# A decoder layer in float32: three pairs of blocks by two levels of Winograd's form in the first pass, weight preparation inside the cross-attention

## The chip, the cores and the metric

The kernel runs on one core of a Trainium2 chip. Its time is the device time of one execution in microseconds, and a comparison takes the median of several runs. The engines of the core work side by side, each through its own instructions in a fixed order: TensorE (PE in the profile, its weight loads PEld), VectorE (DVE), ScalarE (ACT), GpSimd (POOL) and SyncE (SP), which here issues most of the transfers. Transfers can also be issued from ScalarE's and GpSimd's instruction streams.

## The reference

One pre-norm decoder layer on `x` of 16 batches by 128 tokens by 1024 channels, all in float32:

```python
x = x + attn(layernorm(x), Wqkv, bqkv, Wo, bo)         # one head of 256
x = x + xattn(layernorm(x), ctx, ctx, Wq, Wk, Wv, ...)  # linear attention
x = x + ffn(layernorm(x), gate, up, down)               # int4 weights
# xattn: 8 heads of 64
qh = softmax(Wq @ q, axis=-2) * SCALE      # over a head's 64
kh = softmax(Wk @ k, axis=-1)              # over the 1024 positions
context = einsum('bhdn,bhen->bhde', kh, vh)
out = Wo @ einsum('bhde,bhdn->bhen', context, qh) + bo
out = out / max(norm(out), 1e-12) * g * sqrt(128)
# ffn: 1024 -> 2752 -> 1024, weights (nibble - zero) * scale, groups of 64
h = silu(x @ Wg.T) * (x @ Wu.T)
y = h @ Wd.T
```

## The kernel before

The program has three stages in order of time: the self-attention, the cross-attention, and the feed-forward network. The last multiplies with fewer products than the plain way: a matrix product is cut in 2 by 2 quarters and done as seven products of sums of quarters (Winograd's form of Strassen's method) instead of eight.

*Self-attention.* Four tiles of 512 tokens. Beside it, VectorE already prepares feed-forward weights.

*Weight preparation.* `prepare` (L205) is a generator that takes a list of matrices (block, and gate, up or down) and does one step at each `next`. A matrix is two halves. A step on a half is two shifts or masks that take the nibbles (`pa<-raw`), a subtraction of the zero and a multiplication by the scale, both 128x1024. After the second half comes a third step: four 128x512 combinations (`pc`) that form the sums of quarters. The seven results are stored to HBM, from where the feed-forward loads them as `w`; the stores of a step are issued by the following step, on the queue given to `prepare`. `load_raw` (L172) issues the loads of a half ahead of its step. Before, the generator `early` makes gate and up of blocks 0 to 4 in the self-attention, 30 steps, and the generator `rest` makes everything else beside the feed-forward.

*Cross-attention.* Sixteen batches, one after the other, in an order written out by hand: `key_unit` and `query_unit` alternate, and `tick()` after each counts down a list of delayed actions that `later(n, fn)` fills. So everything that follows a unit is placed a set number of ticks behind it. A query unit is two matmuls (`kq`), an exponential on ScalarE (`qe`), a row sum and reciprocal on VectorE (`qden`, `qrec`), a multiplication on GpSimd, a 32x32 transposition on VectorE (`kt`), and a trip through HBM (`kd`, `qs`) that completes the transposition. A key unit is two matmuls, an exponential (`ek`) and two matmuls with the context (`kx`). `mix` forms a batch's small matrix `m_sb`, `project_out` multiplies `qs` with it and normalises with a logarithm and an exponential on ScalarE. `kq` has two PSUM buffers, `qe` and `ek` three buffers each. `note` (L655) adds every row sum and reciprocal to running totals on GpSimd; `raise_flag` tests them at the end, for a fallback that isn't taken here. One instruction, `preload_act_table_set` at L672, loads a ScalarE table that holds logarithm and exponential together.

*Feed-forward.* The tokens are handled in two passes of eight batches. A pass multiplies its 1024 tokens with gate and up, in ten blocks of 256 rows and a smaller last block `RB`, and stores `h` to HBM; both passes' `h` are multiplied with the down weights at the end. `one_block` (L1178) does a block by one level: seven products for gate and seven for up, each four matmuls of 128x512. `two_levels` (L1360) does a pair of blocks by two levels: seven outer products, each of them seven inner products of four matmuls of 128x256, 49 in all for the 28 that two blocks take by one level. VectorE then also has to form the right operands `ti` of each outer product (`inner_right`, four operations, one outer product ahead) and to combine the results (`U`, `V`, `C`); GpSimd forms the left operands `li`. In the order of the outer products, 1, 2, 6, 5, 3, 7, 4, product 7 has the most to combine. In the second pass all five pairs go by two levels, with right operands that are kept; in the first pass only the pairs in `PAIRS` do. A step of `rest` is taken beside most products (`beside`, L1567) and after three of the seven outer products.

The order on each engine: what is wrapped in `InOrder` (L55) stays in the order of the program text, which gives all its instructions the line 63; the rest is placed by the tile framework when the program is built. A tile's buffer is reused when its last reader is done.

In the profile each float32 matmul leaves two records, so a product of four matmuls shows as x8.

Of the kernel before, what the change touches and what calls it, by code (L numbers as in the profile page):

```python
# [18 lines left out]
P = 128  # L19
# [47 lines left out]
def decoder_layer(  # L67
# [95 lines left out]
    def prep_pools(stack, name, c, ahead):  # L163
        for key, bufs in (("a", 3), ("c", c), ("raw", ahead + 1), ("sz", ahead + 1)):
            pools[key] = stack.enter_context(
                tc.tile_pool(name=f"{name}_{key}", bufs=bufs, side="right", reuse_waits="tile")
            )
# [4 lines left out]
    def load_raw(blk, mat, s):  # L172
# [3 lines left out]
        if mat == "d":  # L176
            raw, sz = raw[:w], pools["sz"].tile([P, 2, 512], F32, name="szd")[:w]
            nc.sync.dma_start(raw, dq[ds(start // 2, w), ts(s, 512)])
            for g in range(w // 32):
                row = dsz[start // GROUP + g, ts(s, 1024)].rearrange("(t f) -> t f", t=2)  # L180
                nc.sync.dma_start(sz[ts(g, 32)], row.partition_broadcast(32))
            return raw, *(sz[:, t].unsqueeze(1).to_broadcast([w, 2, 512]) for t in range(2))
# [12 lines left out]
        for m, off, w in parts:  # L195
            q, szs = matrices[m]
            nc.sync.dma_start(raw[:, :, ds(at, w)], q[:, :, ds(off, w)])
            nc.sync.dma_start(
# [6 lines left out]
    def prepare(jobs, ahead, queue, vector=nc.vector):  # L205
# [3 lines left out]
        loads = deque(load_raw(*u) for u in units[:ahead])  # L209
# [6 lines left out]
        for k, (blk, mat, s) in enumerate(units):  # L216
# [6 lines left out]
            if k + ahead < len(units):  # L223
                loads.append(load_raw(*units[k + ahead]))
# [61 lines left out]
    EARLY = 5  # L286

    def give_half(b, h, oT, wo_d, psum, tensor=nc.tensor, vector=nc.vector):
# [19 lines left out]
    prep_pools(first, "q", 4, 1)  # L308
    early = prepare(
        [(blk, mat) for blk in range(EARLY) for mat in "gu"], 1, nc.gpsimd, InOrder(tc, nc.vector)  # L310
    )
    give_pool = ExitStack()
    ag = give_pool.enter_context(tc.tile_pool(name="a_g", bufs=1, reuse_waits="tile"))
    with (
# [166 lines left out]
        for t in range(NT):  # L481
# [38 lines left out]
            else:  # L520

                for i in range(1, BPT):
                    give((t - 1) * BPT + i - 1, oT)
                    value(i, xnT, v)
                atT = turn_weights(at)
# [25 lines left out]
    def block_loads(p, blocks):  # L551

        for n, half in ((0, 0), (1, 0), (1, 1), (0, 1)):
            for i in range(2):
                src = xt_all[p][ds(half * BPT + 2 * i, 2), :, :, :, n]
                tc.keep_in_program_order(
                    nc.sync.dma_start(
# [44 lines left out]
    bcx = unit_pool("b_cx", 2)  # L602
    bw = unit_pool("b_w", 1)
    b0 = unit_pool("b_0", 2)
    bek = unit_pool("b_ek", 3)
    bas = unit_pool("b_as", 1)
    b3 = unit_pool("b_3", 3)
# [4 lines left out]
    bqs = side_pool("b_qs", 5)  # L612
    b1 = side_pool("b_1", 1)
    b2 = side_pool("b_2", 2)
    bps = side_pool("b_ps", 3, space=PSUM)

# [15 lines left out]
    if True:  # L632
        wq_sb = bw.tile([P, HIDDEN], F32, name="wq_sb")
# [7 lines left out]
        sync.dma_start(wk_sb, xwk)  # L641
        sync.dma_start(wq_sb, xwq)
        sync.dma_start(wv_sb, xwv.rearrange("(r p) s -> p r s", p=P))
        sync.dma_start(xwo_sb, xwo.rearrange("(r p) o -> p r o", p=P))
        sync.dma_start(xbo_sb, xbo)
        sync.dma_start(gs_sb, xg)
        vector.tensor_scalar(gs_sb, gs_sb, math.sqrt(S), None, ALU.mult)
        vector.memset(ones, 1.0)
        if plain:

            totals = [bs.tile([P, 2 * HEADS], F32, name=f"total{n}") for n in range(2)]
            for t in totals:
                nc.gpsimd.memset(t, 0.0)

        def note(*both):  # L655
            if plain:
                for t, v in zip(totals, both):
                    t = t[:, : v.shape[1]]
                    nc.gpsimd.tensor_tensor(t, t, v, ALU.add)

        def raise_flag():

            within = [small.tile([P, 1], F32, name=f"within{n}") for n in range(2)]
            for w, t in zip(within, totals):
                vector.tensor_reduce(w, t, AX.X, ALU.add)
                vector.tensor_scalar(w, w, LIMIT, None, ALU.is_le)
            vector.tensor_tensor(within[0], within[0], within[1], ALU.mult)
            ps = bps.tile([P, 1], F32, name="mm")
            tensor.matmul(ps, ones, within[0], start=True, stop=True)
            vector.tensor_copy(flag, ps[0:1])  # L670

        tc.keep_in_program_order(nc.scalar.preload_act_table_set("natural_log_exp_and_others"))  # L672
# [17 lines left out]
        def load_ctx(b):  # L690
            c = bcx.tile([P, C], F32, name="cx")
            sync.dma_start(c, cx[b])
            ct = bct.tile([P, NB, S], F32, name="cxt")
            sync.dma_start(ct, cxt[b])
            return c, ct

        def key_shift(c_sb):

            shift = bas.tile([P, 4, P], F32, name="kshift")
            for oc in range(4):  # L700
# [5 lines left out]
                nmax = small.tile([P, 1], F32, name="knmax")  # L706
# [4 lines left out]
        def key_unit(ctx, p, st):  # L711
# [17 lines left out]
            def use():  # L729
# [16 lines left out]
                if p == 3:  # L746
# [4 lines left out]
                    later(2, lambda: mix(st))  # L751
# [3 lines left out]
        def mix(st):  # L755
# [7 lines left out]
            ksum, krec = (small.tile([P, 4], F32, name=name) for name in ("ksum", "krec"))  # L763
            vector.tensor_copy(ksum, ks)
            vector.reciprocal(krec, ksum)
            note(ksum, krec)
# [17 lines left out]
        def query_unit(xn, pair, qs, wait):  # L784
# [3 lines left out]
            for i in range(2):  # L788
                tensor.matmul(
                    ps[:, i, :], xn[:, ts(2 * pair + i, P)], wq_sb, start=True, stop=True  # L790
# [5 lines left out]
            else:  # L796
                mx = small.tile([P, 2 * HEADS], F32, name="qmx")
# [4 lines left out]
            def weigh():  # L802
                den, rec = (small.tile([P, 2 * HEADS], F32, name=n) for n in ("qden", "qrec"))
# [3 lines left out]
                note(den, rec)  # L807
# [24 lines left out]
        def turned(b):  # L832
# [9 lines left out]
            if b == B - 1:  # L842
                blocks.update(new_blocks(xlate, lambda k: f"X{HB + 2 * k}"))
                loads = block_loads(0, blocks)
                for n in range(8):
                    later(7 + 2 * n, lambda: next(loads))
# [75 lines left out]


        batches = [p + i for p in PASSES for i in range(HB)]
        ctxs = {b: load_ctx(b) for b in batches[:2]}
        wo_again = []
        for d in range(2):
            wo_again.append(bqs.tile([P, C], F32, name="wo_again", tag="qs"))
# [972 lines left out]
```

## Time and profile before

| | |
|---|---|
| median of 3 runs | 2240.34 us (2240.03 to 2240.9) |
| profiled execution | 2241.3 us, its span 2239.5 us |
| TensorE busy | 2204.4 us, 98% of the span, 8330 records |
| VectorE busy | 1482.2 us, 66% |
| ScalarE busy | 468.9 us, 21% |
| GpSimd busy | 553.1 us, 25% |
| moved by DMA | 425.23 MB, 190 GB/s in the mean |
| granted TensorE clock | 0.996 of full speed |

The stages by the times of the span, read from the order of TensorE's instructions: self-attention to 250 us, cross-attention to some 812, with block 0 mixed in from 763 on, blocks 1 to 5 to 1074.5, the pair by two levels to 1163.4, blocks 8 and 9 and the last block to 1297, the second pass to 1760, the down product to the end.

A group's line gives the line of the program, engine, operation, result and operands, shapes and number; then the time of all together, the mean of one in ns; then the idle time of the engine right before them and what ended it. A line of waits gives who waited for whom: total us, times, the longest.

### The profile page before, as it was taken

What the parts mean: (1) busy time and instruction counts of PE and PEld (TensorE: products, weight loads), DVE (VectorE), ACT (ScalarE), POOL (GpSimd) and SP (SyncE); (2) the same over time, 40 slices, a digit from 0 to 9 for tenths busy, and PEclk for the clock granted to TensorE, in tenths of its full rate; (3) what the DMA queues carried; (4) which work ended last, traced back from release to release, by engine and by line L of the source; (5) the groups of instructions that cost most, each with busy time, mean ns of one, the idle gap of its engine ahead of it and who ended that gap; (6) DMA issues with size and microseconds to landing.
All of it is one profiled execution on the core that took longest, in us unless ns stands there. A gap on an engine that the chain in (4) does not pass through costs nothing.

```text
span 2239.5 us, 24114 instructions
## 1 busy us (share of the span) xinstructions
PE 2204.4 (98%) x8330; PEld 1517.3 (68%) x8330; DVE 1482.2 (66%) x2055; ACT 468.9 (21%) x651; POOL 553.1 (25%) x543
## 2 busy tenths in 40 slices
PE   8999899999999999999999999999999999999998
PEld 7556555555555544444774488888887688888887
DVE  6997466667667657666796658787787645544462
ACT  2111135454554431111111112121121000000000
POOL 5452044444444400001320044444442000000000
PEclk9999999999999999999999999999999999999999
DMA  6435246666686768887649834454554964333731
GB/s 251 157 130 169 85 132 198 209 205 197 208 258 192 225 182 287 284 267 253 199 166 301 251 100 158 167 197 155 175 198 165 350 211 164 114 125 129 226 118 39
DMA packets 270835, 425.23 MB, mean 190 GB/s; under 512 B 28784, under 2 KB 130544, under 8 KB 270576
## 3 DMA queue, kind: packets, MB, share of 16 engines
q1 hardware_dynamic: 244624, 377.72, 52.5%
q0 software_dynamic: 8064, 27.27, 3.3%
q10 hardware_dynamic: 18016, 18.62, 2.7%
q8 instruction: 68, 1.11, 0.2%
q14 instruction: 63, 0.52, 0.1%
HBM read 265.62 MB, written 157.35 MB: 189 GB/s over the span
## 4 chain that ended last, share of the span: by engine, by line
PE 90%; DVE 6%; issue 2%; DMA 1%; POOL 1%; ACT 0%; SPq 0%; DVEq 0%; POOLq 0%; ACTq 0%
PE po L1780 21%; PE q L63 20%; PE p L63 18%; PE kq L63 9%; PE mm L63 8%; PE kx L63 5%; PE mm L396 4%; PE mm L411 2%; DVE pa L63 2%; PE p L1157 1%; PE mm L292 1%; PE tr L343 1%; DVE ti L63 1%; DMA wo_again<-in_wo 0%; POOL qe L806 0%
## 5 line engine op out<-in xcount | busy, mean ns | idle before, releaser
L63 PE MATMUL p<-b,w 128*128 128x512 f32 x560 | 248.2, 596 | 1.9 <-DVE sg L63 1.9
L63 PE MATMUL q<-ti,li 128*128 128x256 f32 x1008 | 232.2, 379 | 3.5 <-DVE ti L63 2.8
L63 POOL TENSOR_TENSOR li<-w 128x512 f32<-128x512 f32 x84 | 118.1, 1408 | 433.3 <-DMA w<-wu 244.8
L63 PEld LDWEIGHTS q<-ti,li 128*128 128x128 f32 x1008 | 191.0, 190 | 31.3 <-issue 2.8
L63 PEld LDWEIGHTS p<-b,w 128*128 128x128 f32 x560 | 106.9, 191 | 136.4 <-issue 128.8
L1780 PE MATMUL po<-wc,lc 128*128 128x256 f32 x840 | 183.4, 379 | 0.0
L63 PE MATMUL p<-T,w 128*128 128x512 f32 x400 | 177.2, 592 | 0.0
L1780 PEld LDWEIGHTS po<-wc,lc 128*128 128x128 f32 x840 | 159.6, 190 | 21.8
L63 ACT COPY k<-q 128x512 f32<-128x512 f32 x126 | 73.7, 585 | 399.2 <-PE q L63 399.2
L63 PEld LDWEIGHTS p<-T,w 128*128 128x128 f32 x400 | 76.0, 190 | 95.7 <-issue 95.2
L1780 PE MATMUL po<-wq,lq 128*128 128x256 f32 x560 | 126.7, 379 | 0.2 <-issue 0.2
L806 POOL TENSOR_TENSOR qe<-qe,qrec 128x1024 f32<-128x1024 f32 x64 | 122.0, 1906 | 11.5 <-DVE qrec L63 9.3
L63 PEld LDWEIGHTS mm<-qs,m_sb 128*128 128x128 f32 x512 | 97.3, 190 | 40.1 <-issue 26.8
L63 PE MATMUL kq<-wk_sb,cx 128*128 128x512 f32 x256 | 120.4, 592 | 2.5 <-DMA cx<-in_cx 2.5
L63 PE MATMUL kx<-ek,cxt 128*128 128x512 f32 x256 | 121.8, 598 | 0.0
L63 PE MATMUL mm<-qs,m_sb 128*128 128x256 f32 x512 | 120.8, 379 | 0.0
L63 PE MATMUL kq<-wq_sb,xn 128*128 128x512 f32 x256 | 120.3, 593 | 0.0
L1780 PEld LDWEIGHTS po<-wq,lq 128*128 128x128 f32 x560 | 106.0, 190 | 15.8 <-issue 0.8
L63 DVE TENSOR_TENSOR pa<-pa,sz 128x1024 f32<-128x1024 int32 x86 | 112.6, 1309 | 2.5
L396 PE MATMUL mm<-xnT,wqkv_sb 128*128 128x512 f32 (+1 forms) x320 | 112.9, 509 | 0.0
L63 DVE STREAM_TRANSPOSE kt<-qe 128x1024 f32<-128x1024 f32 x64 | 79.5, 1242 | 43.7 <-POOL qe L806 43.5
L727 ACT ACTIVATE ek<-kq 128x1024 f32<-128x1024 f32 x64 | 65.3, 1020 | 147.4 <-PE kq L63 147.4
(201 smaller groups left out, 3595.7 us busy)
## 6 DMA issues: line engine op xcount, KB each, us to landing
w<-wu SPq DMA_DIRECT2D x140, 256.0 KB, 3.6
lq<-h SPq DMA_DIRECT2D x140, 256.0 KB, 4.4
w<-wg SPq DMA_DIRECT2D x138, 256.0 KB, 2.8
kd<-kt SPq DMA_DIRECT2D x64, 512.0 KB, 2.9
qs<-kd SPq DMA_DIRECT2D x256, 128.0 KB, 3.2
h<-hc SPq DMA_DIRECT2D x80, 256.0 KB, 2.8
wq<-wd SPq DMA_DIRECT2D x70, 256.0 KB, 5.3
h<-h SPq DMA_DIRECT2D x60, 256.0 KB, 3.0
```

What stands on the lines that cost most here:

```text
L63: return lambda *args, **kw: self._tc.keep_in_program_order(fn(*args, **kw))
L292: tensor.matmul(ps, oT[:, d, ts(b % BPT, S)], wo_d[d][:, ts(h, 512)], start=(d == 0), stop=(d == 1),)
L343: nc.tensor.transpose(tr[:, j, :], xn[:, ts(4 * h + j, P)], ident)
L396: nc.tensor.matmul(ps[:, tokens], wqkv_sb[:, f, c, :], xnT[:, c, tokens], start=(c == 0), stop=(c == CC - 1),)
L411: nc.tensor.matmul(ps, xnT[:, c, ts(i, S)], wqkv_sb[:, 4:6, c, :], start=(c == 0), stop=(c == CC - 1),)
L727: nc.scalar.activation(ek, ps, AF.Exp)
L806: nc.gpsimd.tensor_tensor(qe, qe, rec.unsqueeze(2).to_broadcast(wide), ALU.mult)
L1157: tensor.matmul(ps, wt[:, j, :], T[q][:, :, j], start=(first == q and j == 0), stop=(q in (2, 3, 4) and j == JC - 1), skip_group_check=True,)
L1780: nc.tensor.matmul(bank[:, i, :], l[:, ts(i, S)], w,  start=(start and c == 0 and i % 2 == 0), stop=(stop and c == len(pairs) - 1), skip_g ...
```

## The change

- `PAIRS` is [2, 3, 4] instead of [3]: in the first pass blocks 4 to 9 go by two levels, and the one-level blocks are 0 to 3 and the last block.
- The matrices are prepared in another place: gate and up of all blocks first, then the last block's, then the down matrices. 11 matrices instead of 10 in the self-attention, 7 in the cross-attention (new: the generator `middle`, 21 steps, at ticks 3 and 7 of one batch and 5 of the next), 15 beside the feed-forward, with two `pa` buffers instead of three.
- In `two_levels` of the first pass the right operands of outer product 4 are formed during product 3 instead of during product 7, and `ti` has three buffers.
- `note` goes: each row sum has its own column of a tile `sums`, and `raise_flag` takes their maximum and minimum, its matmul four ticks later.
- The table preload goes.
- At the start of the cross-attention the loads are in another order and no longer held in program order, `mix_weights` and `give_half` come some ticks later, and the pools are laid out in another order.
- `mix` runs four ticks after its batch's last key product instead of two; `project_out`'s products one tick later in 13 batches; the first-level operands of the first pass are formed a little later.
- The block loads of the first pass go to ScalarE's queue, the first four weight tiles to GpSimd's; the second pass's block loads are all issued at once after `two_levels` instead of beside blocks 8 and 9.

```diff
-    def prep_pools(stack, name, c, ahead):
-        for key, bufs in (("a", 3), ("c", c), ("raw", ahead + 1), ("sz", ahead + 1)):
+    def prep_pools(stack, name, a, ahead):
+        for key, bufs in (("a", a), ("c", 4), ("raw", ahead + 1), ("sz", ahead + 1)):
...
-    EARLY = 5
+    todo = [(blk, mat) for blk in range(RB) for mat in "gu"] + [(RB, "r"), (RB, "m")]
+    todo += [(blk, "d") for blk in range(len(BLOCKS))]
+    EARLY, MIDDLE = 11, 18
...
+                    next(early, None)
...
-    def block_loads(p, blocks):
+    def block_loads(p, blocks, queue=nc.sync):
...
+    prep_pools(sides, "x", 2, 1)
+    middle = prepare(todo[EARLY:MIDDLE], 1, nc.gpsimd, vector, sync)
...
-        sync.dma_start(wk_sb, xwk)
-        sync.dma_start(wq_sb, xwq)
...
+        nc.sync.dma_start(wk_sb, xwk)
+        ctxs = {batches[0]: load_ctx(batches[0])}
+        wo_again = []
+        for d in range(2):
+            wo_again.append(bqs.tile([P, C], F32, name="wo_again", tag="qs"))
+            nc.sync.dma_start(wo_again[d], wo[ts(d, P)])
+        nc.sync.dma_start(wq_sb, xwq)
...
+        ctxs[batches[1]] = load_ctx(batches[1])
...
-            totals = [bs.tile([P, 2 * HEADS], F32, name=f"total{n}") for n in range(2)]
-            for t in totals:
-                nc.gpsimd.memset(t, 0.0)
-
-        def note(*both):
-            if plain:
-                for t, v in zip(totals, both):
-                    t = t[:, : v.shape[1]]
-                    nc.gpsimd.tensor_tensor(t, t, v, ALU.add)
+            sums = bs.tile([P, B * 4 * 2 * HEADS + B * 4], F32, name="sums")
...
-        tc.keep_in_program_order(nc.scalar.preload_act_table_set("natural_log_exp_and_others"))
...
-                    later(2, lambda: mix(st))
+                    later(4, lambda: mix(st))
...
-                loads = block_loads(0, blocks)
+                loads = block_loads(0, blocks, nc.scalar)
                 for n in range(8):
-                    later(7 + 2 * n, lambda: next(loads))
+                    later(4 + 3 * n, lambda: next(loads))
...
-        mix_weights()
+        later(4, mix_weights)
...
-                when = (13, 14, 15, 16, 17, 1, 1)
+                when = (14, 15, 16, 17, 18, 1, 1) if k < 13 else (13, 14, 15, 16, 17, 1, 1)
...
+            for n in ((3, 7), (5,))[k % 2] if k < 14 else ():
+                later(n, lambda: next(middle, None))
...
-            prep_pools(second, "f", 4, 2)
...
+            prep_pools(second, "f", 2, 2)
+            rest = prepare(todo[MIDDLE:], 2, nc.sync, vector)
...
-        PAIRS = [3]
+        PAIRS = [2, 3, 4]
...
-                            bufs=1 if self.kept else 2,
+                            bufs=1 if self.kept else 3,
...
-                if not last:
+                if not last and not (ps == 0 and q == 7):
                     right.extend(operands.inner_right(OUTERS[n + 1][1]))
+                if ps == 0 and q == 3:
+                    extra.extend(operands.inner_right(OUTERS[n + 2][1]))
...
-            load_weights(nc.gpsimd if n == 0 else nc.sync)
+            load_weights(nc.gpsimd)
...
                 if blk == 0:
-                    steps = 1
+                    steps = n == 13
                 elif blk == RB:
-                    steps = n in (0, 2, 4)
+                    steps = n < 4
                 else:
-                    steps = (1, 1 + (mat == "g" and blk < 3), 1, 0, 1, 0, 0)[n % 7]
+                    steps = (1, 1 + (mat == "g"), 1, 0, 1, 0, mat == "u")[n % 7]
...
-            if pass1 and n % 3 == 0:
-                next(pass1_loads, None)
...
-                pass1_loads = block_loads(1, pass1)
+                for _ in block_loads(1, pass1):
+                    pass
```

## The prediction

> **What bounds the kernel now.** I read the first part of the page, then the stages in windows of my own cut, then what TensorE waited for, then the groups of the other engines.
>
> ```profile
> PE 2204.4 (98%) x8330; PEld 1517.3 (68%) x8330; DVE 1482.2 (66%) x2055; ACT 468.9 (21%) x651; POOL 553.1 (25%) x543
> ```
>
> TensorE is busy all but 35 us of the span, so a change gains by taking work off TensorE, or by filling those 35 us. The windows give, after length, the busy time of PE, PEld, DVE, ACT and POOL, then clock, DMA share and GB/s:
>
> ```profile
> 250.00:292.00 42.00, 36.29 (x96) 16.60 (x95) 13.61 (x28) 11.96 (x14) 3.11 (x4) 0.96 0.28 100
> 720.00:760.00 40.00, 37.82 (x142) 21.71 (x142) 29.94 (x38) 17.44 (x21) 14.67 (x22) 1.00 0.50 158
> 760.00:853.00 93.00, 87.74 (x227) 43.76 (x227) 56.23 (x81) 32.12 (x43) 13.17 (x17) 0.96 0.76 235
> ...
> 448.00:479.00 31.00, 31.00 (x109) 17.70 (x108) 21.56 (x29) 15.91 (x19) 13.46 (x16) 1.00 0.68 203
> ...
> 900.50:948.50 48.00, 48.00 (x113) 21.28 (x112) 29.95 (x43) 5.72 (x11) 0.00 (x0) 1.00 0.83 265
> 1098.70:1110.80 12.10, 12.10 (x58) 10.65 (x57) 10.49 (x14) 2.72 (x4) 5.44 (x4) 1.00 0.59 186
> 1123.30:1136.60 13.30, 12.61 (x58) 10.49 (x57) 13.09 (x17) 1.76 (x3) 5.69 (x4) 1.00 0.41 126
> 1148.70:1163.40 14.70, 12.27 (x57) 10.46 (x56) 12.97 (x19) 2.70 (x4) 1.26 (x1) 1.00 0.32 106
> 1211.00:1259.00 48.00, 48.00 (x113) 21.28 (x112) 29.92 (x42) 5.79 (x10) 0.00 (x0) 1.00 1.03 314
> ```
>
> One batch of the cross-attention takes 31.2 us with TensorE full and VectorE free for 9.6. A block by one level takes 48.0 us, TensorE full, even where the DMA engines moved 314 GB/s (the last row). The outer products of the one pair by two levels take 12.10 us where nothing waits; some take 13.30 and 14.70, where VectorE was busy to the end. TensorE's waits:
>
> ```profile
> PE p L1157 <- DMA w<-wg: 4.9, 1, 4.9
> PE q L63 <- DVE ti L63: 3.3, 4, 2.4
> PE mm L63 <- DMA wo_again<-in_wo: 3.1, 1, 3.1
> PE kq L63 <- DMA cx<-in_cx: 2.5, 1, 2.5
> PE p L63 <- DVE sg L63: 1.9, 1, 1.9
> ```
>
> And the rows that price what moves:
>
> ```profile
> L63 DVE TENSOR_TENSOR pa<-pa,sz 128x1024 f32<-128x1024 f32 x43 | 59.0, 1373 | 1.3
> L63 DVE TENSOR_TENSOR pa<-pa,sz 128x1024 f32<-128x1024 int32 x43 | 53.6, 1246 | 1.2
> L659 POOL TENSOR_TENSOR total<-total,qden 128x16 f32<-128x16 f32 x64 | 43.9, 686 | 135.5 <-DVE qden L63 135.5
> L806 POOL TENSOR_TENSOR qe<-qe,qrec 128x1024 f32<-128x1024 f32 x64 | 122.0, 1906 | 11.5 <-DVE qrec L63 9.3
> L877 ACT ACT_TABLE_LOAD x2 | 2.6, 1283 | 0.0
> ```
>
> **The change, part by part.** The terms go against the profiled execution: 2241.3 us, span 2239.5 and 1.8 around it, 1.0 above the median 2240.34.
>
> *Pairs 2 and 4 by two levels.* A pair by one level is 28 products of 3.43 us: two windows of 48.0, 96.0 us. By two levels it is 49 products of 1.73 us: seven times 12.10, 84.7; pair 3 took 1074.5 to 1163.4, 88.9, the rest being waits for `ti`. Before, the three pairs cost 88.9 + 2 x 96.0 = 280.9. Unhindered: 254.1, a gain of 26.8. With pair 3's waits in each: 266.7, a gain of 14.2. VectorE fits on average: its seven windows in pair 3 sum to 75 us, three preparation steps included. The edit to the right operands forms those of the last outer product (q=4) one outer product earlier. The 2.4 us wait, at q=4, goes. But four more `ti` (0.7 to 1.1 us each, some 3.3) now fall into q=3, whose window holds 13.09 us of VectorE already; that is what is late next. In the built program's order the `6` operand of q=7 stands behind two of them: 1139.3 plus 1.4 is 1140.7, and TensorE wants it at 1140.0. So 0.6 us appears where 2.4 went, and the small waits before it (0.9) stay: 1.5 us a pair, 86.2 x 3 = 258.6. **-22.3**. Worst end: the 3.3 us all exposed and the old wait kept, 92.2 x 3, a gain of 4.3. GpSimd's left operands (5.4 us per outer product) fit in 12.1.
>
> *Seven matrices prepared in the cross-attention.* A step of `prepare` is two shifts at 0.457, two 128x1024 at 1.246 and 1.373: 3.5 us; every third step is four 128x512 at about 0.7: 2.8. Three steps cost 9.9, the 21 steps 69 us of VectorE, alternately two and one a batch. A batch with two has 21.6 + 7.0 = 28.6 of 31.2 us, so TensorE stays the bound; the cover is 2.6 us thin. The late readers got slack too: `mix` runs two ticks later, the `qs` products one (3.9 us). If VectorE can't use its longest gap (5.8 us, waiting for the `ksum` product), a two-step batch needs 34.4, 3.2 too many, x 7 = 22. Low end 0, since TensorE has nothing to gain there. Nearest is the full window: **+2**. Their 28 loads stand in SP's order before `kd` and `qs`, 0.5 us each; their 49 stores take 0.56 us each on GpSimd, 27 us, where the running totals (81 us of GpSimd) are gone. Both fit: GpSimd has 13.5 of 31, and the added 18 MB make 203 GB/s into some 245.
>
> *The table preload is gone.* In the built program each batch's logarithm and exponential now bring a table load each, 28 for the first 14 batches; before, one served them all. At 1.283 us: 35.9 us of ScalarE, 2.6 a batch on 15.9 of 31.2. Behind the first load queue the logarithms, the exponential and the next `ek`, which frees a bank. I follow one batch: the `sq` product's first half ends at 0.9; load to 2.6, logarithms to 3.8, load to 5.1, exponential to 6.2, `ek` to 7.2; that bank is wanted again at 12.3. **0**; the other end is all exposed, +36. No gain: TensorE was full.
>
> The Trainium skill, "ScalarE: Activation LUTs", sections "Table sets: the hidden batching unit" and "What ACT_TABLE_LOAD costs", speaks against this edit: logarithm and exponential share one set, and a switch is put at 2.66 us with its drain. The trace shows 1.283, with the next activation 0.01 us behind it at 813.2. By the page's price 28 switches would be 74 us of ScalarE (an estimate), still beside TensorE if hidden, and 2286 us if none were.
>
> *The start of the cross-attention.* TensorE idles 5.7 us of 250 to 292, mostly for `cx` and `wo_again`, which queued behind eight transfers. Now `wk`, `cx`, `wo_again` go first and `mix_weights` later. Between -5.7 and +1 (three more early steps beside the last `value` products: 9.9 us of VectorE where it is busy 16.0 of 31): **-4**.
>
> *The start of the feed-forward.* 7.4 us idle in 720 to 853, 4.9 of it for the first `w`. The first tiles move from SP to GpSimd: eight triggers at 0.59 us, seven of them ahead of one `qe` multiplication; their buffers now lie on the key tiles, free a batch sooner. Behind them that `qe`, and so `kt` and `qs`, may be 4.1 us later, covered by block 0's products. Between -7.4 and +4.1, nearest to the 4.9 row: **-5**. The block loads move to ScalarE (8 x 0.4 us; waiting for `xt` stores they would hold `ek`); as eight triggers they fit in its 12 us free a batch: 0. The flag's two reductions read 1088 columns, about 1.2 us each by the nearest VectorE row (`qden`, 1.19): beside products, 0.
>
> *Blocks 1 to 3.* Ten steps instead of eight: 30 + 6 = 36 of 48 us; with two `pa` buffers instead of three a matrix's first step may wait about 2.5 us for a store, some 8 a block: 44. 0; high end +5.
>
> *Second-pass blocks.* All eight loads (4.2 MB) start at the end of the two levels instead of beside blocks 8 and 9, so the last block's 38 us alone cover them: at 200 GB/s 21 us. **+0.5**; high end +6, for three 2.6 us operands now behind them.
>
> Sum: -22.3 + 2 - 4 - 5 + 0.5 = -28.8; 2241.3 - 28.8 = 2212.5, about 2211.5 as a median. I say **2212**.
>
> **Rivals.** (a) VectorE bounds the cross-attention: the 22 us worked out, 20 above my 2. For it: 28.6 of 31.2, and an order fixed in advance. Against it: the gap can be filled, since the step stands at another tick. 2232. (b) The three pairs stall as at the worst end, 4.3 instead of 22.3: 2230. For it: q=3's extra `ti`. Against: the average of 75 in 84.7. (c) The other side: the table loads come onto TensorE's path, in the `ek` wait at the end of each batch, two banks being all there are. All exposed: 2248. It decides from 28 us, 2.0 a batch, on. Against it: 5 us between `ek` and its bank's next use. (d) The pairs are hidden anyway: excluded while TensorE is full in the one-level blocks.
>
> **How the numbers follow.** Chances: forecast 0.69, (a) 0.12, (b) 0.11, (c) 0.08. The range is 2203 (both starts and the pairs at their good ends: 2241.3 - 26.8 - 5.7 - 7.4 + 2, then -1) to 2234, which takes in (a) and (b). A measurement tells 0.2% (4.5 us) from no change. Faster takes the forecast's 0.69 and 0.18 of the 0.23 of (a) and (b), which are 0.3 to 0.5% faster alone; the 0.05 where they meet goes to same (0.04) and slower (0.01), beside (c)'s 0.08: faster 0.87, same 0.04, slower 0.09.
>
> **What would show it.** Right: PE records near 8330 + 2 x 168 = 8666; three pairs in 256 to 262 us; batches still 31.2 with VectorE near 27 in the mean; ScalarE some 36 us of loads; no `w` wait. Wrong: batches with two steps longer than 31.5 (a), `q` waits for `ti` above 3 us a pair (b), `kq` waiting for `ek` (c), or a wait for `b` at the second pass's start.

## The result, and the profile after

The changed kernel takes 2262.97 us (median of 3 runs, 2261.18 to 2263.22) against 2240.34 (2240.03 to 2240.9): a ratio of 1.0096, 95% interval [1.0078, 1.0114]. It is slower; 2212 was predicted, with a range to 2234. The profiled execution of it has a span of 2259.3 us, 19.8 longer than the one before.

The first part of the page, after (busy time, share of the span, instructions):

```profile
PE 2191.6 (97%) x8666; PEld 1584.5 (70%) x8666; DVE 1620.3 (72%) x2185; ACT 514.9 (23%) x691; POOL 632.5 (28%) x499
```

The records of TensorE are the 8666 foretold and its busy time fell by 12.8 us, so the work did go. What grew is idle time. Stages of the kernel after, in windows (length; busy us of PE, PEld, DVE, ACT, POOL; clock, DMA share, GB/s):

```profile
250.00:290.00 40.00, 40.00 (x110) 18.55 (x110) 18.25 (x34) 12.66 (x14) 6.08 (x7) 1.00 0.39 136
448.00:479.00 31.00, 31.00 (x109) 17.72 (x108) 26.68 (x34) 18.50 (x21) 13.50 (x9) 1.00 0.76 237
598.00:730.00 132.00, 117.11 (x379) 66.52 (x378) 93.80 (x122) 64.42 (x74) 46.44 (x33) 0.95 0.78 239
776.00:860.00 84.00, 71.62 (x190) 36.68 (x191) 34.28 (x51) 29.48 (x38) 10.94 (x13) 0.94 0.60 178
903.20:951.20 48.00, 48.00 (x113) 21.21 (x113) 35.19 (x49) 5.79 (x10) 0.00 (x0) 1.00 1.01 300
951.20:1006.00 54.80, 50.57 (x115) 21.94 (x114) 42.44 (x56) 5.97 (x10) 7.21 (x4) 0.97 1.01 315
1094.70:1183.70 89.00, 85.52 (x387) 74.05 (x386) 80.02 (x95) 16.81 (x26) 41.12 (x28) 0.98 0.43 140
```

In order: the start of the cross-attention is full, where 5.7 us were idle. A batch beside the preparation is full with VectorE at 26.7 of 31. Four batches in the middle have 15 us idle. Block 0 has 12 idle. A block with ten preparation steps is full in 48.0; the window of the next one (block 3) has 4.2 idle. A pair by two levels takes 89.0. TensorE's waits, after (total, times, longest):

```profile
PE mm L63 <- DMA qs<-kd: 14.9, 4, 6.6
PE p L1161 <- DVE h L63: 11.2, 1, 11.2
PE tr L344 <- ACT xn L152: 9.3, 1, 9.3
PE q L63 <- DVE ti L63: 8.2, 6, 2.4
PE p L63 <- DVE sg L63: 3.3, 1, 3.3
PE q L63 <- ACT k L63: 2.8, 4, 0.7
PE p L1161 <- DMA w<-wg: 2.8, 1, 2.8
PE p L63 <- DVE h L63: 2.3, 2, 1.4
```

The first two are new and come to 26.1 us. The third lies in the first 10 us of the kernel; before, it was 9.4, so of the 35 idle us that the prediction counted, 9.4 were out of the change's reach. To see what each stage costs, I set marks that every kernel has, in us from the span's start: block 0's first product; the first copy `k` of block 1; the end of block 3 (the first product of the two levels; before, where block 4 follows, block 4's first copy `k` less its product of 3.4); the first copy `k` of the last block; the end. The names E1 to E12 are those of the experiments below.

| | block 0 | block 1 | end of block 3 | last block | end |
|---|---|---|---|---|---|
| before | 762.7 | 833.9 | 978.6 | 1263.2 | 2239.5 |
| after | 776.7 | 858.4 | 1005.6 | 1279.1 | 2259.3 |
| E1 block loads on SP | 754.6 | 837.7 | 984.3 | 1254.8 | 2232.1 |
| E3 first tiles on SP | 775.9 | 846.2 | 991.3 | 1263.7 | 2243.5 |
| E5 both | 754.6 | 823.8 | 968.5 | 1240.6 | 2220.2 |
| E6 both, three `pa`, old `ti` | 754.2 | 823.2 | 964.2 | 1237.9 | 2216.3 |
| E9 both, step moved | 754.5 | 823.7 | 969.7 | 1237.5 | 2228.7 |

From before to after the stages changed by +14.0, +10.5, +2.5, -11.1 and +3.9: 19.8 in all.

The experiments ran on several chips, on which the kernel before took 2240.69 to 2242.02 us; each ratio is against the kernel before on the same chip.

### The profile page after: what moved, and what is told of

Same layout as the page of the kernel before. It is cut to its first block, busy times and chain, and to the rows that moved or that the text cites. A ratio compares the mean times of both kernels' runs of the same rounds, so it can differ in the third digit from the quotient of the medians.

```text
span 2259.3 us, 24919 instructions
## 1 busy us (share of the span) xinstructions
PE 2191.6 (97%) x8666; PEld 1584.5 (70%) x8666; DVE 1620.3 (72%) x2185; ACT 514.9 (23%) x691; POOL 632.5 (28%) x499
## 4 chain that ended last, share of the span: by engine, by line
PE 84%; DVE 9%; DMA 3%; issue 3%; POOL 1%; ACT 1%; SPq 0%; DVEq 0%; POOLq 0%; ACTq 0%
PE q L63 25%; PE po L1787 21%; PE kq L63 9%; PE p L63 8%; PE mm L63 7%; PE kx L63 5%; PE mm L397 4%; PE p L1161 2%; DVE pa L63 2%; PE mm L412 2%; DVE ti L63 2%; PE mm L295 1%; DMA b<-xt 1%; DVE C L63 1%; DMA wd<-pc 1%
## 5 line engine op out<-in xcount | busy, mean ns | idle before, releaser
L63 PE MATMUL q<-ti,li 128*128 128x256 f32 x1344 | 312.3, 381 | 10.2 <-DVE ti L63 7.3
L63 PEld LDWEIGHTS q<-ti,li 128*128 128x128 f32 x1344 | 255.7, 191 | 48.5 <-POOL li L63 12.7
L63 POOL TENSOR_TENSOR li<-w 128x512 f32<-128x512 f32 x112 | 164.2, 1469 | 253.5 <-DMA wd<-pc 146.6
L63 ACT COPY k<-q 128x512 f32<-128x512 f32 x168 | 98.2, 585 | 538.4 <-PE q L63 538.4
L820 POOL TENSOR_TENSOR qe<-qe,qrec 128x1024 f32<-128x1024 f32 x64 | 156.7, 2448 | 158.5 <-DVE qrec L63 141.2
L63 PE MATMUL p<-b,w 128*128 128x512 f32 x304 | 136.1, 600 | 5.6 <-DVE sg L63 3.3
L63 PE MATMUL mm<-qs,m_sb 128*128 128x256 f32 x512 | 124.8, 388 | 14.9 <-DMA qs<-kd 14.9
L63 POOL TENSOR_TENSOR li<-w,li 128x512 f32<-128x512 f32 x56 | 76.6, 1367 | 212.5 <-PE q L63 179.1
L63 PE MATMUL q<-b,w 128*128 128x256 f32 x512 | 122.2, 382 | 0.0
L63 PEld LDWEIGHTS p<-b,w 128*128 128x128 f32 x304 | 58.0, 192 | 79.2 <-issue 70.0
L63 DVE TENSOR_TENSOR C<-q,k 128x512 f32<-128x512 f32 x120 | 82.2, 685 | 39.0 <-PE q L63 36.8
```

The costliest lines, as they stand in the source:

```text
L63: return lambda *args, **kw: self._tc.keep_in_program_order(fn(*args, **kw))
L820: nc.gpsimd.tensor_tensor(qe, qe, rec.unsqueeze(2).to_broadcast(wide), ALU.mult)
```

## The experiments

**The block loads (E1, E2, E4).** The four waits for `qs` fall at 608 to 695 us, where the block loads, moved to ScalarE's queue, were started (590.7 to 684.2). The waits of SP's own queue there, kernel after, 598 to 700 us:

```profile
SPq L63 <- DMA b<-xt: 36.0, 5, 9.3
SPq L63 <- DMA kd<-kt: 27.9, 9, 6.7
```

SP does not start these loads any more, and nothing that it starts there reads `b`. In the trace every transfer that SP or ScalarE starts raises one of the same eight counters (semaphores) when it lands, and GpSimd's raise eight others. In the kernel after, seven of the eight block loads landed 0.01 to 0.02 us before SP went on from a wait for the counter of that very load. That is theory A. E1 undoes the edit:

```diff
-                loads = block_loads(0, blocks, nc.scalar)
+                loads = block_loads(0, blocks)
                 for n in range(8):
-                    later(4 + 3 * n, lambda: next(loads))
+                    later(7 + 2 * n, lambda: next(loads))
```

> The changed kernel with one edit undone: the eight block loads go back to SP's queue, at ticks 7 + 2n as before. Theory A (shared completion counters): in the built program the DMAs of SP and of ScalarE take the same eight counters in turn, GpSimd's have eight of their own; a 512 KB block load started on ScalarE, 6.5 us in flight, holds whichever SP trigger takes its counter next, and SP is in order. That gave TensorE the 14.9 us of waits for qs between 606 and 695 us and the slow clock behind them. A expects no wait for qs above 1 us, the stage 598 to 730 shorter by 15 to 20 us and a time of 2243 to 2248 against 2263. Theory B (traffic): the block loads meet the loads and stores of the middle preparation, which were not there before, and the transfers are late whatever starts them. B expects 10 us or more of waits for qs to stay, and 2259 to 2267. The wait of 11.2 us in block 0 and the rest stay in both.

E2 keeps the ticks and changes the queue alone:

```diff
-                loads = block_loads(0, blocks, nc.scalar)
+                loads = block_loads(0, blocks, nc.gpsimd)
```

> The changed kernel with the eight block loads on GpSimd's queue at its own ticks 4 + 3n: same transfers at nearly the same times, other counters. A (shared counters of SP and ScalarE): the waits for qs go as in the run with SP's queue, 2243 to 2249; SP no longer waits for b. B (traffic, or the moment of the loads): they stay, 10 us or more, 2259 to 2267. GpSimd gives 8 x 0.6 us, which its 13 us of work in a batch of 31 can take; a trigger that waited for xt there would hold the qe multiplication, which would show as waits of VectorE for qe.

E4 is the kernel before with this one edit of the change:

```diff
-                loads = block_loads(0, blocks)
+                loads = block_loads(0, blocks, nc.scalar)
                 for n in range(8):
-                    later(7 + 2 * n, lambda: next(loads))
+                    later(4 + 3 * n, lambda: next(loads))
```

> The kernel before with one edit of the change alone: the eight block loads on ScalarE's queue at ticks 4 + 3n. No middle preparation here. A (shared counters): waits of TensorE for qs appear between 600 and 700 us, 8 to 16 us with the slow clock, 2249 to 2260 against 2240. B (traffic with the middle preparation): no such wait, 2237 to 2243.

E1 took 2236.77 us, E2 2240.72, beside 2241.37 for the kernel before on that chip: ratios 0.9982 [0.9973, 0.9992] and 1.0 [0.999, 1.0009]. Both lie under A's ranges, by 6 and 2 us. In both no wait for `qs` is left; block 0 begins 22.1 us sooner than after with E1 and 21.7 with E2. E1's span fell by 27.2; the rest lies in later stages, which the edit doesn't touch, and isn't followed. The stage of the four batches in E1:

```profile
598.00:730.00 132.00, 132.00 (x458) 75.84 (x457) 113.94 (x142) 77.65 (x89) 55.58 (x38) 1.00 0.84 259
```

It moves more data (259 GB/s against 239) and TensorE is full: theory B, traffic, falls. E1 undoes the ticks with the queue; E2 settles that it was the queue, and which property of it, since the loads have the same ticks, and landed no sooner (a median of 7.3 us against 6.5). SP's longest waits in E2, same window:

```profile
SPq L63 <- DMA kd<-kt: 55.6, 13, 8.9
SPq L63 <- DMA cxt<-in_cxt: 1.7, 1, 1.7
```

None for `b`. So it is the sharing of counters between SP and ScalarE that makes SP, which works in order, wait for a load that it has nothing to do with. The Trainium skill, "DMA: Bandwidth & Descriptors", section "Why a DMA increments its semaphore by 16 and not by 1", gives a reason for such a wait: when two DMAs in flight share a semaphore, a wait for it can pass before the first has landed. No run here shows that hazard; that two queues share counters, and what the wait costs, is shown by these traces.

E4 took 2246.55, ratio 1.0026 [1.0016, 1.0036], 5.2 us over before, with one wait for `qs` of 3.4 us (its profiled execution is the fastest of its nine, 2244.25). The mechanism is there without the preparation (SP waits 30.6 us for `b` between 570 and 730 us), but A's 8 to 16 us are missed. What differs is how far SP is ahead. E4 first, over that window, with the wait for `kt`, that is for data not yet made:

```profile
...
SPq L63 <- DMA b<-xt: 30.6, 5, 9.7
SPq L63 <- DVE kt L63: 22.2, 9, 5.6
```

and the kernel after:

```profile
...
SPq L63 <- DMA b<-xt: 46.9, 6, 10.8
...
SPq L63 <- DVE kt L63: 0.4, 2, 0.2
```

Beside the preparation SP has no such slack. That the 28 loads of the preparation took it fits the waits for `kt` over that window in the kernel before (32.5 us) and in E1 (16.5), but is argued, not tried.

**The first weight tiles (E3, E5).** The other new wait, of 11.2 us, ends block 0. VectorE's rows there, kernel after:

```profile
812.69 1.25 DVE L63 STREAM_TRANSPOSE kt<-xn 128x1024 f32<-128x1024 f32 x1 [1.04 <-ACT xn L152]
837.45 1.23 DVE L63 SCALAR_TENSOR_TENSOR y<-sq,y 128x1024 f32<-128x1024 f32 x1 [23.51 <-ACT sq L891]
...
848.30 0.69 DVE L63 TENSOR_TENSOR h<-p,k 128x512 f32<-128x512 f32 x1
849.02 0.69 DVE L63 TENSOR_TENSOR h<-h,sg 128x512 f32<-128x512 f32 x1
```

and TensorE's answer:

```profile
849.04 5.86 PE L1161 MATMUL p<-b,w 128*128 128x512 f32 x8 [11.20 <-DVE h L63]
```

VectorE waits 23.5 us for the last batch's norm, in order, and the `h` that frees a PSUM bank stands behind it. Among the rows left out, between that norm and this `h`, are the flag's two reductions (845.4 to 848.2 us): some 2.9 of the 11.2 us stand behind them. In TensorE's order the last sum for the norm comes after 12 products of block 0, where before there were not quite 9 (the 14 in the expectation below is a miscount). E3 undoes the edit that I suspected:

```diff
-            load_weights(nc.gpsimd)
+            load_weights(nc.gpsimd if n == 0 else nc.sync)
```

> The changed kernel with one edit undone: of the first four weight tiles only the first is started by GpSimd, the other three by SP, as before. Theory C: seven triggers ahead of a qe multiplication on GpSimd make the last batch's key and query tiles late in the builder's own order, so that block 0's products are put ahead of the last batch's last products (the sums for its norm stand behind 14 products instead of 9), VectorE, in order, waits 23.5 us for that norm, and h behind it frees the PSUM bank 11.2 us late. C expects that wait under 2 us; against it the first wait for w may grow from 2.8 to 5: 2251 to 2256. Theory D: the 11.2 us come from the missing table preload, from mix two ticks later or from the flag's two reductions of 1.25 us: the wait stays above 8 us, 2260 to 2266. The 14.9 us of waits for qs stay in both.

E3 took 2243.73, ratio 1.0008 [0.9998, 1.0018]. From block 0's first product to block 1 it needs 70.3 us (before 71.2, after 81.7), and no wait for `h` at that place is left; the first `w` is waited for 3.9 us instead of 2.8. Theory C holds, though the time lies 7 us under its range. The span fell by more than that, 15.8 us: 2.1 of it in blocks 1 to 3 and 1.5 after them, which I haven't followed.

E5 has both edits of the queues undone.

> The changed kernel with the two edits of the queues undone together: the eight block loads on SP at ticks 7 + 2n, and of the first weight tiles only the first on GpSimd. Singly they gave 20.6 us up to the first product of block 0, and 12.2 us from there to block 1. If the two are separate causes they add: 2222 to 2228, no wait for qs and none for h above 4 us. If they share a part (the same late tiles of the last batch), 2230 to 2236.

E5: 2222.25, ratio 0.9911 [0.9895, 0.9928]. Block 0 begins 22.1 us sooner than after, as with E1, and block 1 comes 12.5 us sooner after that (E3: 11.4; by these marks, not by the 20.6 and 12.2 of the expectation). The two causes add, and without them the change is faster than the kernel before, by 0.9%.

**Blocks 1 to 3, and the early right operands (E6).** In block 3 VectorE's preparation steps waited for stores (kernel after):

```profile
970.67 0.76 DVE L63 TENSOR_SCALAR pa<-raw 128x512 int32<-128x512 int32 x2 [4.29 <-DMA wd<-pa]
```

```profile
975.20 12.26 PE L63 MATMUL p<-b,w 128*128 128x512 f32 x24 [3.35 <-DVE sg L63]
```

E6 is E5 with:

```diff
-            prep_pools(second, "f", 2, 2)
+            prep_pools(second, "f", 3, 2)
...
-                            bufs=1 if self.kept else 3,
+                            bufs=1 if self.kept else 2,
...
-                if not last and not (ps == 0 and q == 7):
+                if not last:
                     right.extend(operands.inner_right(OUTERS[n + 1][1]))
-                if ps == 0 and q == 3:
-                    extra.extend(operands.inner_right(OUTERS[n + 2][1]))
```

> The run before this one (both queue edits undone) with two more edits undone, each read from its own stage: three buffers for pa in the later preparation instead of two, and the right operands of the inner products as before (two buffers of ti, none formed early; both fit in memory only together). Blocks 1 to 3: theory E, a preparation step at the head of VectorE's order waits 1.8 to 5.5 us for the store of wd from the same buffer, and sg and h behind it stop TensorE: with three buffers these waits and the 3 to 7 us of block 3 go. Rival: ten steps instead of eight fill VectorE, and they stay. Pairs: theory F, the early operands only moved the 2.4 us wait from the last outer product to the one before, since three ti there took 1.7 us beside GpSimd's li instead of 0.7: each pair stays within 0.5 of 88.5 us. Rival, as predicted: a pair becomes 2 to 3 us longer without them. E with F: 5 us less than the run before, 2217 to 2222.

E6 took 2219.57, ratio 0.9907 [0.989, 0.9923]. From block 1 to the end of block 3: 141.0 us against 144.7 in E5, and the waits for `sg` and `h` there (3.3 us in E5) are gone. E11, below, has the same three `pa` and needs 141.1 us, without these waits: theory E holds. (The medians of E5 and E6 differ by 2.7 us, less than E6's runs among themselves; the stages tell more than the time.) From there to the last block: 273.7 against 272.1, so the early operands were worth 0.5 us a pair in this setting, as theory F had it.

**The pairs (E7, E9, E11).** E7 is E5 with `PAIRS = [3]`.

> Both queue edits undone and only pair 3 by two levels, as in the kernel before; blocks 4, 5, 8 and 9 by one level. By the windows of the changed kernel (88.5 us a pair, of which 3.5 are waits, against 96.0) the other two pairs are worth 15 us: 15 more than the run with both edits undone. By the prediction (86.2, with the third pair's gain inside) 19.6 us. If the one-level blocks beside the preparation stall too, more than 20.

E7: 2229.29 us, 7.0 over E5 by the medians, 11.2 by the spans (E7's profiled execution lies 3.9 over its median): less than the 15 expected. The reason stands in its only pair. No wait for `ti` above 0.2 us is listed in it, and it took 86.2 us (134.3 from block 5's first copy to block 8's, less a block of 48.1), the figure predicted for each pair. No row of `pa` lies in that stage: the later preparation was over by then. Its seven outer products, in windows:

```profile
1067.50:1079.60 12.10, 12.10 (x58) 10.65 (x57) 4.75 (x7) 1.86 (x4) 3.80 (x3) 1.00 0.39 119
1079.60:1091.70 12.10, 12.10 (x58) 10.65 (x57) 5.80 (x9) 2.36 (x5) 5.07 (x4) 1.00 0.30 95
1091.70:1103.80 12.10, 12.10 (x58) 10.65 (x57) 10.48 (x14) 2.73 (x5) 5.41 (x4) 1.00 0.38 128
...
1115.90:1128.00 12.10, 12.10 (x58) 10.65 (x57) 8.36 (x12) 1.77 (x4) 5.08 (x4) 1.00 0.28 89
1128.00:1140.10 12.10, 11.43 (x53) 9.44 (x52) 11.89 (x14) 2.54 (x4) 6.03 (x4) 1.00 0.28 91
```

VectorE (third busy figure) is light in the first two and has 8.4 in q=3 (the 1115.9 window). With a preparation step there it had 12.4 of 12.6 us (E1, 1032.4 to 1045). E9 moves that step:

```diff
-                    0, PAIRS, first_operands, lambda q: q in (1, 6, 5) and next(rest, None)
+                    0, PAIRS, first_operands, lambda q: q in (1, 6, 4) and next(rest, None)
```

> Both queue edits undone, and in the three pairs the preparation step that stands after outer product 5 moved to after outer product 4, so that it falls into the next pair's first outer product (7.4 us of VectorE in 12.1) and not into that of q=3 (12.4). In the run with one pair by two levels no preparation was left beside it, and it took 86.2 us with no wait for ti. Theory H: the preparation step beside the extra ti is what makes VectorE late; TensorE's waits for ti fall from 8.8 us to under 3, a pair from 89 to 86.3 to 87, and the time by 5 to 8 us: 2214 to 2218. Rival: VectorE is full in the pair as a whole (77.7 of 87.3 us) and the step's delay is only moved: waits above 6 us, 2219 to 2224.

E9 took 2231.16, ratio 0.9959 [0.9946, 0.9973]: 9 us more than E5. Both sides were wrong, in different places. The waits for `ti` did fall to 1.1 us, but a pair gained little: from the end of block 3 to the last block 267.8 us against 272.1, and the second pair took 88.4, not 86.3 to 87. Against 84.7 for seven full outer products, the waits that the view lists are 1.9 us of the difference; the rest lies in products that followed each other at 1.8 to 1.9 us instead of 1.73, behind waits too short for the list or behind a wait. The loss is in the last block. SP, VectorE and TensorE, E9:

```profile
1238.34 11.92 SPq L559 DMA_DIRECT2D b<-xt  x8
...
1252.55 1.73 SPq L214 DMA_DIRECT2D wd<-pa  x3
```

```profile
1259.14 0.76 DVE L63 TENSOR_SCALAR pa<-raw 96x512 int32<-96x512 int32 x2 [13.69 <-DMA wd<-pa]
```

```profile
1280.39 5.14 PE L63 MATMUL p<-b,w 128*128 128x512 f32 x8 [12.04 <-DVE h L63]
```

The moved step's store stood in SP's order behind the eight block loads of the second pass. E12 takes these off SP:

```diff
-                for _ in block_loads(1, pass1):
+                for _ in block_loads(1, pass1, nc.gpsimd):
```

> The run with the moved step and two pa buffers, with one more edit: the eight block loads of the second pass, which the change starts all at once at the end of the two levels, go to GpSimd's queue, idle there. In the run with the moved step they held SP for 11.9 us at 1238 us; the moved step's store of wd stood behind them, the next preparation step waited 13.7 us for it at the head of VectorE's order, and h behind it gave TensorE a wait of 12.0 us in the last block. Theory I: SP's order is the cause; without the eight triggers the store goes 12 us sooner, the wait falls under 2 us, and the time by 10 to 14 us: 2216 to 2222. Rival: the transfers themselves (4.2 MB beside the stores) make the store late, whatever queue starts them: the wait stays above 8 us, 2228 to 2234.

E12: 2220.6, ratio 0.9909 [0.9893, 0.9926]; the wait in the last block is 1.5 us. Theory I holds: the loads took as long to land (a median of 7.6 us, in E9 7.7), but the store that ends VectorE's wait was started at 1242.6 us instead of 1253.4, and the wait is 4.7 us instead of 13.7. That store was longer in flight (7.7 us against 5.7), so the loads, which GpSimd started some 13 us sooner than SP had, may slow it, but by less than the order had cost.

E10 and E11 stand on E9. E10 has its loss in the last block (a wait for `h` of 11.9 us), E11 a part of it (4.3). E10:

```diff
-            prep_pools(second, "f", 2, 2)
-            rest = prepare(todo[MIDDLE:], 2, nc.sync, vector)
+            prep_pools(second, "f", 3, 1)
+            rest = prepare(todo[MIDDLE:], 1, nc.sync, vector)
```

> The run before this one with three buffers for pa in the later preparation, paid for in memory with loads one unit ahead instead of two. Blocks 1 to 3, theory E (the store of wd that a step waits for): waits for sg and h of some 3.4 us go, 2 to 4 us less than the run before, 2211 to 2216. Rival: with one load ahead the steps wait for raw and szd instead, and sg and h wait as long or longer: no gain, or 2 to 6 us more.

It took 2234.55, ratio 0.9976 [0.9967, 0.9985], and the waits in block 3 are 0.9 us for `sg` and 2.9 for `h`, as long as in E9 (0.8 and 2.2). VectorE's steps now wait for `raw` and `szd` (13.1 and 8.3 us between 820 and 1006 us): the rival holds. A third `pa` pays only with two loads ahead, as in E6.

E11 is E9 with the edits of E6.

> Both queue edits undone, the step moved, three buffers for pa, and the right operands as in the kernel before (two buffers of ti, none formed early). It prices the early operands alone, with no preparation step in q=3. If they are worth what the prediction gave them, a wait of 2.4 us for ti stands at the last outer product of each pair and a pair takes 88 to 89 us: 5 to 7 us more in the pairs than with the early operands (2214 to 2221). If the step was all there was to it, a pair takes 86.3 to 87 in this form too and the time is that of the run with the three buffers, 2211 to 2216.

E11 took 2229.45, ratio 0.9949 [0.9935, 0.9963], over both of its ranges. The stage of the pairs is 277.0 us against 267.8 in E10: with no step in q=3 the early operands are worth 3.1 us a pair. A wait of 3.3 us for `ti` is back at two of the three last outer products, and of 2.2 at the third.

**The table loads (E8).** E8 is E5 with

```diff
+        tc.keep_in_program_order(nc.scalar.preload_act_table_set("natural_log_exp_and_others"))
         later(4, mix_weights)
```

> Both queue edits undone and the table preload put back, so that the logarithms and exponentials of the first 14 batches share one table and 28 loads of 1.283 us (36 us of ScalarE) go. The prediction put them at nothing, TensorE being full there: within 1.5 us of the run with both edits undone, and no wait of TensorE for ScalarE goes. Rival (c) of the prediction: they hold ek or the norm, and 3 us or more come back.

E8: 2226.04 (2221.84 to 2229.84), ratio 0.9936 [0.9919, 0.9952]. ScalarE's busy time fell from 513.6 to 480.0 us, and the spans differ by 0.2 (2220.0 and 2220.2). The 27 loads that go by the trace (36 in E5, 9 in E8) cost nothing that shows; the medians differ by 3.8 us the other way, less than E8's runs among themselves.

## Why the prediction was wrong

- **The block loads on ScalarE** were put at 0, as eight triggers in 12 us of free ScalarE. This is the step that failed: it counted the time of the engine that starts the loads and not the queue that is coupled to it. What the runs showed in its place: SP, which shares its counters with ScalarE, waited for the loads, and so `qs` came late. By E1 that cost 22.1 us up to block 0 (21.7 by E2, which changes the queue alone), of which 14.9 are the four waits and some 6.5 slow products after three of them.
- **The start of the feed-forward** was put at -5, the worst end at +4.1. The first `w` did come sooner (2.8 us instead of 4.9), but seven triggers ahead of a `qe` on GpSimd were said to be "covered by block 0's products". They were not, since the builder put these products in front of the last batch's, and the norm behind them held VectorE and through it a PSUM bank: 11.4 us by E3. The prediction followed the late tile to TensorE and not to VectorE's order. The flag's two reductions, put at 0 "beside products", stood in that order too.
- **The pairs** were put at -22.3 and gave 11.1. The mechanism was right (E7 has a pair of 86.2), the size was off: 89 to 92 beside the preparation. The mis-sized term is the extra `ti`, put at 0.7 to 1.1 us each, and the 0.6 us wait that followed from it: 2.4, measured, in every pair. That is 5.4 of the 11.2 us missed here; 1.9 more are slow products behind two of these waits, and the rest isn't followed. By E7 and E9 the wait needs the preparation step as well: without it beside them no wait for `ti` over 0.3 us is left. The rows, kernel after, VectorE and then GpSimd:

```profile
1069.49 0.69 DVE L63 TENSOR_TENSOR ti<-b 128x512 f32<-128x512 f32 x1
1070.09 1.76 DVE L63 TENSOR_TENSOR ti<-T 128x512 f32<-128x512 f32 x1
1071.77 1.75 DVE L63 TENSOR_TENSOR ti<-b,ti 128x512 f32<-128x512 f32 x1
1073.44 0.68 DVE L63 TENSOR_TENSOR ti<-T,ti 128x512 f32<-128x512 f32 x1
```

```profile
1069.65 1.65 POOL L63 TENSOR_TENSOR li<-w,li 128x512 f32<-128x512 f32 x1 [4.49 <-PE q L63]
1071.31 1.66 POOL L63 TENSOR_TENSOR li<-w 128x512 f32<-128x512 f32 x1
```

  The two `ti` that start while GpSimd is at an `li` take 1.75 us and each end 0.55 us after that `li`; the one that starts before the first `li` and the one after the second take 0.7. TensorE's wait of 2.43 ends at 1073.66. The kernel before had such rows too (1.75 us at 1091.23 and 1125.39), which a mean of 1.1 hides. The Trainium skill, "Trainium Architecture — The Big Picture", section "What this means for kernel authors", states that VectorE and GpSimd share a port by an exclusive lock; these rows agree, and give the price: 1.06 us an operation here.
- **Blocks 1 to 3**: 0 with a high end of 5; measured +2.5. The stores that two `pa` buffers wait for were foreseen (8 us a block, held to fit); in block 3 they didn't fit (E6: 3.7 us).
- **The start of the cross-attention**: -4, and +2 for the preparation in it. Right in sign, and too small: in E1 block 0 begins 8.1 us sooner than before, 2.0 of it the `w` wait. Batches stayed at 31.2 us, VectorE at 27.0 in the mean of three. Rival (a) didn't come.
- **The table loads**: 0. Right (E8); rival (c), the only one on the slow side, didn't come either. The slow side came from two terms that no rival named.
- **Second-pass blocks**: +0.5 with a high end of 6. Measured +3.9 after the last block's first copy, 3.3 in E5. 1.7 of it lie in the last block, behind a wait of 1.4 us for `h` that E6, with three `pa`, doesn't have; the other 2.2 are not taken apart. E9 shows the danger in it: the eight loads at once hold SP for 12 us.

The terms missed 31.5 us up to block 1, 2.5 in blocks 1 to 3, 11.2 in the pairs and 3.4 after them: the 48.6 between -28.8 and +19.8. (The low end of the range, by its own sum, is 2202 and not 2203; nothing hangs on it.)

## What to carry to other kernels

When a transfer is moved to another queue, look in the built program's waits at which counters the two queues share, and at which queue waits for a completion that is none of its business; only then is the new queue free. An engine that works in order is late with everything behind the one instruction that waits, so a trigger or a step that "fits in the average" has to be followed to the next instruction on its engine and to who waits for that. Undoing the two queue edits turned 1.0% slower into 0.9% faster: with a bundle, read each stage against marks that both kernels have, before judging the whole.

## What the runs showed beside this

After a wait TensorE's products are slow for a while, and not always: three waits for `ti` of 2.42 or 2.43 us in the kernel after were followed by the same group of 8 in 1.97, 2.41 and 3.46 us. The windows right behind them show the granted clock, third figure from the end:

```profile
1073.60:1076.00 2.40, 2.34 (x11) 2.11 (x12) 2.40 (x5) 1.25 (x2) 0.22 (x1) 1.00 0.02 6
1162.60:1165.00 2.40, 2.34 (x9) 2.04 (x10) 2.40 (x5) 1.06 (x1) 0.00 (x0) 0.80 0.00 0
1253.10:1256.60 3.50, 3.43 (x9) 2.85 (x10) 3.50 (x6) 1.06 (x1) 0.00 (x0) 0.56 0.00 0
```

In the trace's own record the granted clock falls to 0.50 seven times between 600 and 1260 us, each time in one of the waits of over 2.3 us or up to 1.4 us after it, for 3.41 us or two or three times that. The Trainium skill, "TensorE: Matmul & The Clock Gate", section "Part 1: The HAM clock gate", puts the loss of the clock at an idle window of some 3.4 us that runs free of the program; the length of the falls agrees, but here waits shorter than that were enough in two of these three cases. So a wait here cost up to 2.8 us more than its length (the one of 6.6 us for `qs`), which the prediction's sum had left out.
